# Edges of an attention kernel copied into PSUM by VectorE instead of transposed on TensorE, with other places for its rounds

## The chip, the core and the metric

The kernel runs on one core of a Trainium2 chip, in one launch. The metric is the device time of a run in microseconds (us), and the number to compare is the median of several runs. A profile is one execution, with every instruction's start and length; its span goes from the first instruction to the last.

## The reference

A graph network of four layers on N = 3327 nodes with 128 features, each `x = layernorm(x + layer(x, adj))`. The change touches layer 0, an attention with 128 "batches" d and 8 channels h, where the edge matrix is added to every score:

```python
q = (x @ Wq.T).reshape(d, n, h)          # d = 128, h = 8; k and v alike
a = jnp.einsum('dnh,dmh->dnm', q, k) * d ** -0.5
a = a + adj + adj                        # spatial and edge encoding are both adj
a = jax.nn.softmax(a, axis=2)
out = jnp.einsum('dnm,dmh->dnh', a, v)
```

So there are 128 matrices of 3327 x 3327 scores to be exponentiated; layers 1 to 3 are multiplications with `adj` and its transpose.

## The kernel before

A first stage projects queries, keys and values and writes them to DRAM. The attention stage does layer 0. A last stage does the output projection and layers 1 to 3.

**Blocks.** In attention the queries are cut into 7 chunks of CW = 476 columns (the last one overlaps), the 26 tiles of 128 keys into four sets of 7, 7, 6 and 6 (`KBS`). A chunk with a key set is a block, 28 in all, in the order of chunks. A block goes through d = 0 to 127, in 32 groups of four heads (`GROUP`).

**Scores.** For each d the tiles of the block are done in three sets (`SETS`): 3, 2, 2 tiles of a seven-tile block, 2, 2, 2 of a six-tile block. Each set has its own PSUM banks (`sc`, one buffer each, a bank a tile; seven of the eight banks in all). Scores are not made anew for each d: the bank is never cleared within a block, and the matmul of d adds q_d k_d and takes off q_(d-1) k_(d-1). So the edges are put into the banks once a block, ahead of d = 0, and stay. `exponents` (from L594) does one set: at d = 0 it first transposes the edges into the bank with TensorE (L603), from `e_in`, which has queries in rows; then come the scores (L610); then ScalarE takes the exponential of the whole set in one instruction (L618) into a tile `e0`, `e1` or `e2` of SBUF, with 6, 7 and 8 buffers.

**Help.** In some groups (`on_vector`) VectorE does the exponential of the third set at the group's first d, as a polynomial in ten instructions (`vector_exp`, L574 to L580). The first reads PSUM at once; the others wait in a list `vec`, from which `vector_work` takes some at each place, by a clock of planned costs.

**Rounds.** `weigh` (L624) multiplies one key tile's exponentials of four heads with the values (L635), four matmuls side by side, into the eighth bank `o`. The rounds of a group, 7 or 6, are done during the next group. A group has twelve places, numbered d % 4 times 3 plus the set; a tuple of `PLACES` (L452) lists the places at which rounds follow, and there is one tuple for each g % 4. A round of a third set waits for the polynomial of its group. Every third group, `flush` lets VectorE add `o` into SBUF (L646, L648).

**Order.** In this stage TensorE, ScalarE, VectorE and GpSimd work in program order (`manual_schedule`). `prepare` loads keys and queries two groups ahead on the SP queue (`load_heads`, three buffers), and at d % 4 of 0 or 1 lists the copies of queries for the next group (`copy_queries`, L499 to L501). `load_edges` (L429) loads the edges of the next block at d = 0 of this one, in two DMAs on SP, into the one buffer of `e_in`.

**Background.** While attention runs, the last stage's transposed matrix `adjT_s` is made: every eighth group (`PACE`) a piece of `adj` is loaded on SP, turned by VectorE in blocks of 32 (`piece_work`) and stored by GpSimd's queue (`piece_store`, L234). Row block t of `adjT_s` holds, for the queries of tile t, keys in partitions: the turned edges. Pieces go by four query tiles at a time, tiles 4 on first and tiles 0 to 3 last.

Of the kernel before, what the change touches and what calls it, by code (L numbers as in the profile page):

```python
# [10 lines left out]
F32 = mybir.dt.float32  # L11
# [8 lines left out]
P = 128  # L20
GROUP = 4
# [3 lines left out]
PACE = 8  # L25
CW = 476
# [24 lines left out]
def kernel(ctx: ExitStack, tc: tile.TileContext, x, adj, wq, wk, wv, wo,  # L51
# [14 lines left out]
    nc = tc.nc  # L66
    N, D = x.shape
# [3 lines left out]
    NP = T * P  # L71
# [8 lines left out]
    KBS = [(0, 7), (7, 7), (14, 6), (20, 6)]  # L80
# [40 lines left out]
    adjT_s = scratch.tile([T * P, T * P], F32, name="adjT_s")  # L121
# [123 lines left out]
    with tc.tile_pool(name="pw", bufs=1) as pw, tc.tile_pool(name="pa", bufs=2) as pa, \  # L245
# [12 lines left out]
        for u in range(NU):  # L258
            base, R, full, rest = spread(u)
# [96 lines left out]
        d = 0  # L356
# [52 lines left out]
    def attention():  # L409
        with tc.tile_pool(name="acc", bufs=1) as accp, tc.tile_pool(name="kq", bufs=3) as kq, \  # L410
# [12 lines left out]
            subs = [(j, min(P, CW - j)) for j in range(0, CW, P)]  # L423

            blocks = [(min(c, N - CW), kb) for c in range(0, N, CW) for kb in range(len(KBS))]
            groups = [(b, g) for b in range(len(blocks)) for g in range(NHG)]
            steps = [(b, d) for b in range(len(blocks)) for d in range(D)]

            def load_edges(b):  # L429
                c0, kb = blocks[b]  # L430
                k0, nt = KBS[kb]
                w = min(nt * P, N - k0 * P)
                e = ed.tile([P, len(subs), 7 * P], F32, name="e_in")
                if w < nt * P:
                    nc.gpsimd.memset(e[:, :, w:nt * P], 0.0)
                nf = CW // P
                nc.sync.dma_start(out=e[:, 0:nf, 0:w],
                                  in_=flat_ap(adj, c0 * N + k0 * P, [[N, P], [P * N, nf], [1, w]]))
                nc.sync.dma_start(out=e[0:CW - nf * P, nf, 0:w],
                                  in_=flat_ap(adj, c0 * N + (nf * P * N + k0 * P), [[N, CW - nf * P], [1, w]]))  # L440
                return e


            SETS = {7: [(0, 3), (3, 2), (5, 2)], 6: [(0, 2), (2, 2), (4, 2)]}

            def on_vector(nt, g):

                return g % 4 != 3 if nt == 7 else g % 2 == 0

            PLACES = {7: ((0, 0, 4, 7, 7, 10, 10), (0, 0, 4, 7, 7, 9, 10), (1, 1, 4, 6, 8, 10, 10),  # L452
                          (0, 2, 3, 5, 7, 8, 10)),
                      6: ((0, 0, 3, 6, 8, 10), (0, 2, 4, 5, 7, 9)) * 2}

            def load_heads(b, g):

# [62 lines left out]
            heads, values, pairs, edges, es, stores = {}, {}, {}, {}, {}, []  # L520


            pieces = [(u, c) for u in [*range(1, NU), 0] for c in range(NPC)]
            loaded, worked, turning = [], [], []

            def background(n):
                if n % PACE == 0 and worked:
                    piece_store(pe, *worked.pop(0))
                if n % PACE == 0 and pieces:
                    u, c = pieces.pop(0)  # L530
                    loaded.append((u, c, piece_load(pe, u, c)))

            def background_work(n):
                if n % PACE == 3 and loaded:
# [6 lines left out]
                if n % PACE == 7 and turning:  # L541
                    clock[1] += 2.4
                    for _ in turning.pop():
                        pass
# [38 lines left out]
            clock = [0.0, 0.0]  # L583
# [10 lines left out]
            def exponents(b, d, si):  # L594
                kb = blocks[b][1]
                nt = KBS[kb][1]
                t0, n = SETS[nt][si]
                s = sc[si]
                if d == 0:
                    for i in range(n):  # L600
                        tl = tile_at(nt, t0 + i)[2]
                        for j, (q0, w) in enumerate(subs):
                            nc.tensor.matmul(s[:, i, q0:q0 + w], lhsT=edges[b][0:w, j, tl * P:(tl + 1) * P],  # L603
                                             rhs=ident[0:w, 0:w], is_transpose=True,
                                             start=(j == 0), stop=True, skip_group_check=True)
                kt, qt = heads[b, d // GROUP]
                k = d % GROUP
                for i in range(n):
                    rg, pos, _ = tile_at(nt, t0 + i)
                    nc.tensor.matmul(s[:, i, 0:CW], lhsT=kt[64 * rg:64 * rg + 64, k, pos * P:(pos + 1) * P],  # L610
                                     rhs=qt[64 * rg:64 * rg + 64, k, :],
                                     start=False, stop=True, skip_group_check=True)
                e = ex.tile([P, (3, 2, 2)[si], CW], F32, tag=f"e{si}", name=f"e{si}", bufs=(6, 7, 8)[si])
                if on_vector(nt, d // GROUP) and (d % GROUP, si) == (0, 2):
                    vector_exp(e[:, 0:n, :], s[:, 0:n, 0:CW], (b, d // GROUP))
                    clock[1] += 1.2
                else:
                    nc.scalar.activation(e[:, 0:n, :], s[:, 0:n, 0:CW], AF.Exp, scale=2.0)  # L618
                for i in range(n):
                    es[b, d, t0 + i] = e[:, i, :]  # L620
                if d == 0 and si == len(SETS[nt]) - 1 and b + 1 < len(blocks):
                    edges[b + 1] = load_edges(b + 1)

            def weigh(b, g, r):  # L624

                k0, nt = KBS[blocks[b][1]]
                tl = tile_at(nt, r)[2]
                m = tokens(k0 + tl)
                u = g % PACK

                while any(of == (b, g) for _, of, _ in vec) and r >= SETS[len(queue_of)][2][0]:
                    vec.pop(0)[2]()
                for j in range(GROUP):
                    c = 32 + (tl * GROUP + j) * 32 - u * A1
                    nc.tensor.matmul(o[32 * j:32 * j + 32, 0:CW], lhsT=values[b, g][:m, c:c + 32],  # L635
                                     rhs=es[b, g * GROUP + j, r][:m, :],
                                     start=(r == 0 and u == 0), stop=(r == nt - 1),
                                     skip_group_check=True)
                if r == nt - 1 and (u == PACK - 1 or g == NHG - 1):
                    flush(b, g // PACK)  # L640
# [20 lines left out]
            queue, place = [], 0  # L661
            with tc.manual_schedule(engines={mybir.EngineType.PE, mybir.EngineType.Activation,
                                             mybir.EngineType.Pool, mybir.EngineType.DVE}):
                edges[0] = load_edges(0)
# [472 lines left out]
    with tc.manual_schedule(engines={mybir.EngineType.PE, mybir.EngineType.SP}):  # L1137
# [18 lines left out]
        for t in range(T):  # L1156
            n = tokens(t)
# [87 lines left out]
```

## Time and profile before

| what | value |
|---|---|
| median of 3 runs | 10919.42 us (10911.48 to 10927.48) |
| the profiled execution, its own time | 10915.5 us |
| its span | 10913.7 us |
| first stage / attention / last stage | 334.9 / 9806.6 / 772.2 us |
| exponentials on ScalarE, L618 | 10192, mean 1076 ns |
| exponentials on VectorE, L574 | 560, mean 1150 ns |
| rounds' matmuls, L635 | 46592 records, mean 573 ns |
| scores' matmuls, L610 | 23296, mean 439 ns |
| edges' transposes, L603 | 728, median 272 ns |
| granted TensorE clock | 0.995 |

The page gives busy time for each engine and each group of instructions, and ahead of a group the idle time of its engine with what ended it. Lengths of matmuls and of exponentials overlap in time, so a rate is read from start to start. The timeline lists instructions in order of time, merged where they follow each other, with the idle time before them.

### The profile page before, as it was taken

What the parts mean: (1) busy time and instruction counts of PE and PEld (TensorE: products, weight loads), DVE (VectorE), ACT (ScalarE), POOL (GpSimd) and SP (SyncE); (2) the same over time, 40 slices, a digit from 0 to 9 for tenths busy, and PEclk for the clock granted to TensorE, in tenths of its full rate; (3) what the DMA queues carried; (4) which work ended last, traced back from release to release, by engine and by line L of the source; (5) the groups of instructions that cost most, each with busy time, mean ns of one, the idle gap of its engine ahead of it and who ended that gap; (6) DMA issues with size and microseconds to landing.
All of it is one profiled execution on the core that took longest, in us unless ns stands there. A gap on an engine that the chain in (4) does not pass through costs nothing. (4 is left out here: it accounts for less than half of the span.)

```text
span 10913.7 us, 202710 instructions
## 1 busy us (share of the span) xinstructions
PE 10590.0 (97%) x76941; PEld 4114.5 (38%) x76941; DVE 8351.7 (77%) x9359; ACT 9774.0 (90%) x10671; POOL 1667.9 (15%) x2742
## 2 busy tenths in 40 slices
PE   8899999999999999999999999999999999999999
PEld 5333333333333333333333333333333333333779
DVE  6788778887788877788877888778887788777312
ACT  3799999999999999999999999999999999999400
POOL 0111122111221111211112111121111100001200
PEclk9899999999999999999999999999999999999999
DMA  7888888888888888888888888888888888788676
GB/s 252 155 127 123 129 133 133 128 124 127 136 133 128 124 127 131 136 123 127 131 131 135 115 122 121 123 133 129 126 129 123 120 119 117 116 111 118 209 283 245
DMA packets 995063, 1516.19 MB, mean 139 GB/s; under 512 B 202471, under 2 KB 812577, under 8 KB 980267
## 3 DMA queue, kind: packets, MB, share of 16 engines
q1 hardware_dynamic: 896854, 1371.75, 77.5%
q0 software_dynamic: 79616, 116.88, 4.7%
q8 instruction: 623, 10.21, 0.5%
q10 hardware_dynamic: 17620, 14.49, 0.4%
q14 instruction: 350, 2.87, 0.1%
HBM read 1371.86 MB, written 130.35 MB: 138 GB/s over the span
## 5 line engine op out<-in xcount | busy, mean ns | idle before, releaser
L618 ACT ACTIVATE e<-sc 128x952 f32<-128x952 f32 (+1 forms) x10192 | 9551.3, 1076 | 281.1 <-PE sc L610 274.7
L635 PE MATMUL o<-e,v_pad 128*32 128x476 f32 (+1 forms) x46592 | 5657.5, 573 | 47.1 <-DVE acc L648 39.8
L610 PE MATMUL sc<-qt,kt 64*128 64x476 f32 x23296 | 4503.2, 439 | 178.4 <-ACT e L618 113.1
L610 PEld LDWEIGHTS sc<-qt,kt 64*128 64x128 f32 x23296 | 2197.0, 184 | 4570.9 <-ACT e L618 4015.0
L580 DVE SCALAR_TENSOR_TENSOR e<-e,ey 128x952 f32<-128x952 f32 x1680 | 1932.7, 1150 | 52.3
L515 POOL COPY v_pad<-vs 128x192 f32<-128x192 f32 (+1 forms) x896 | 534.4, 622 | 7986.1 <-DMA vs<-v_img 5559.1
L635 PEld LDWEIGHTS o<-e,v_pad 128*32 128x32 f32 (+1 forms) x46592 | 1027.9, 108 | 1904.7 <-issue 1858.7
L574 DVE TENSOR_SCALAR ey<-sc 128x952 f32<-128x952 f32 x560 | 643.9, 1150 | 1047.2 <-PE sc L610 1041.2
L501 DVE CAST qt<-qt 64x1904 fp32r<-64x1904 f32 x896 | 1032.8, 1153 | 30.4
L499 DVE TENSOR_SCALAR qt<-qt 32x1428 fp32r<-32x1428 f32 x896 | 807.6, 901 | 159.2 <-DMA qt<-q_s 100.6
L234 POOL DMA_DIRECT2D adjT_s<-at x1352 | 785.3, 587 | 234.5 <-DMA adjT_s<-at 162.2
L580 DVE SCALAR_TENSOR_TENSOR e<-e,et 128x952 f32<-128x952 f32 x560 | 647.5, 1156 | 17.8
L576 DVE SCALAR_TENSOR_TENSOR ey<-et,ey 128x952 f32<-128x952 f32 x560 | 645.1, 1152 | 19.4
L580 DVE SCALAR_TENSOR_TENSOR e<-ey 128x952 f32<-128x952 f32 x560 | 642.0, 1146 | 0.0
L1081 PE MATMUL bank<-y,eT 128*128 128x128 f32 (+1 forms) x4056 | 473.9, 276 | 0.4 <-DVE h L1203 0.4
L1081 PEld LDWEIGHTS bank<-y,eT 128*128 128x128 f32 (+1 forms) x4056 | 465.3, 192 | 5.7 <-DVE h L1203 0.6
L648 DVE TENSOR_TENSOR acc<-o,acc 128x476 f32<-128x476 f32 x231 | 150.3, 651 | 312.4 <-PE o L635 312.0
L575 DVE TENSOR_SCALAR et<-ey 128x952 f32<-128x952 f32 x560 | 372.6, 665 | 18.7
L577 DVE TENSOR_SCALAR et<-et 128x952 int32<-128x952 int32 x560 | 371.1, 663 | 19.3
L500 DVE TENSOR_SCALAR qt<-qt 32x476 fp32r<-32x476 f32 x896 | 360.2, 402 | 7.8 <-DMA qt<-lead_s 3.5
L1041 ACT ACTIVATE rstd<-mv,eps 128x1 f32<-128x1 f32 x104 | 30.4, 293 | 265.5 <-DVE mv L1039 265.5
L655 POOL DMA_DIRECT2D o_s<-acc x308 | 191.4, 625 | 34.9 <-DVE acc L648 22.0
(152 smaller groups left out, 2402.6 us busy)
## 6 DMA issues: line engine op xcount, KB each, us to landing
kt<-k_s SPq DMA_DIRECT2D x5320, 96.0 KB
kt<-k_s SPq DMA_DIRECT2D x1764, 128.0 KB
eT<-adjT_s SPq DMA_DIRECT2D x78, 1664.0 KB
qt<-q_s SPq DMA_DIRECT2D x896, 119.0 KB
qt<-q_s SPq DMA_DIRECT2D x1792, 59.5 KB
vs<-v_img SPq DMA_DIRECT2D x224, 224.0 KB
adjT_s<-at POOLq DMA_DIRECT2D x1352, 32.0 KB, 6.0
vs<-v_img SPq DMA_DIRECT2D x224, 192.0 KB
```

Source lines behind the costliest of these rows:

```text
L234: nc.gpsimd.dma_start(out=flat_ap(adjT_s, (t * P + 32 * q) * NP + c * PIECE, [[NP, 32], [P, ns], [1, P]]), in_=at[32 * i:32 * i + 32].rear ...
L499: return [(0.9, None, lambda: nc.vector.tensor_scalar(qt[32:64, 1:], qf[0:32, 0:GROUP - 1], -1.0, None, ALU.mult)), (0.4, None, lambda: nc ...
L501: (1.2, None, lambda: nc.vector.tensor_copy(qt[64:128], qf[0:64]))]
L515: nc.gpsimd.tensor_copy(vp[:, 32:32 + nt * GROUP * 32].rearrange("p (x c) -> p x c", c=32)[:, :, 0:H], vs.rearrange("p (x c) -> p x c", c=H))
L574: nc.vector.tensor_scalar(y, x, -58 * math.log(2.0), 2 / math.log(2.0), ALU.max, ALU.mult)
L575: vec.append((0.7, of, lambda: nc.vector.tensor_scalar(t, y, ROUND, None, ALU.add)))
L576: vec.append((1.2, of, lambda: nc.vector.scalar_tensor_tensor(y, t, ROUND, y, ALU.subtract, ALU.subtract)))
L580: vec.append((1.2, of, lambda i=i, a=a: nc.vector.scalar_tensor_tensor(e, e if i else y, a, t if i == len(POLY) - 1 else y, ALU.add, ALU.m ...
L610: nc.tensor.matmul(s[:, i, 0:CW], lhsT=kt[64 * rg:64 * rg + 64, k, pos * P:(pos + 1) * P], rhs=qt[64 * rg:64 * rg + 64, k, :], start=False ...
L618: nc.scalar.activation(e[:, 0:n, :], s[:, 0:n, 0:CW], AF.Exp, scale=2.0)
L635: nc.tensor.matmul(o[32 * j:32 * j + 32, 0:CW], lhsT=values[b, g][:m, c:c + 32], rhs=es[b, g * GROUP + j, r][:m, :], start=(r == 0 and u = ...
L1081: nc.tensor.matmul(ps[:n, 0:D], lhsT=e[:m, s, :n], rhs=y[:m, s, col:col + D], start=(s == 0), stop=(s == T - 1))
```

## The change

- From the third chunk on (blocks 8 to 27) edges come from `adjT_s`, keys in partitions, and `put_edges` lets VectorE copy them into the banks: three copies a tile, since the chunk doesn't begin at a tile of queries. TensorE's transposes stay for blocks 0 to 7.
- `load_edges` loads one part of the next block's edges at a time, at d = 0, 8, 16, 24 and 32. `e_in` has five row blocks instead of four, `e2` seven buffers instead of eight.
- `on_vector`: of seven-tile groups those with g % 4 of 1, 2, 3 have help (before 0, 1, 2), of six-tile groups the odd ones (before the even ones). As many as before.
- `PLACES` is new; `FIRST` holds for the first group of blocks 1 to 7.
- The background's load and store move from n % 8 = 0 to 2, its work from 3 to 4 and from 7 to 0 of the groups' number.

```diff
-            def load_edges(b):
+            def turned(b):
+                return b >= 2 * len(KBS)
+
+            def put_edges(b, s, i, tl):
+                e = edges[b].rearrange("p t (s n) -> p t s n", n=P)
+                a = blocks[b][0] % P
+                full = (CW + a - P) // P
+                nc.vector.tensor_copy(s[:, i, 0:P - a], e[:, 0, tl, a:P])
+                nc.vector.tensor_copy(s[:, i, P - a:P - a + full * P].rearrange("p (t n) -> p t n", n=P),
+                                      e[:, 1:1 + full, tl, :])
+                rest = CW - (P - a) - full * P
+                if rest:
+                    nc.vector.tensor_copy(s[:, i, CW - rest:CW], e[:, 1 + full, tl, 0:rest])
+                clock[1] += 0.6
+
+            def load_edges(b, j):
...
+                if j == 0:
+                    edges[b] = ed.tile([P, 5, 7 * P], F32, name="e_in")
+                if turned(b):
+                    t = c0 // P + j
+                    if t * P < c0 + CW:
+                        nc.sync.dma_start(out=edges[b][:, j, 0:nt * P],
+                                          in_=flat_ap(adjT_s, t * P * NP + k0 * P, [[NP, P], [1, nt * P]]))
+                    return
...
-                return g % 4 != 3 if nt == 7 else g % 2 == 0
+                return g % 4 != 0 if nt == 7 else g % 2 == 1
...
-            PLACES = {7: ((0, 0, 4, 7, 7, 10, 10), (0, 0, 4, 7, 7, 9, 10), (1, 1, 4, 6, 8, 10, 10),
-                          (0, 2, 3, 5, 7, 8, 10)),
-                      6: ((0, 0, 3, 6, 8, 10), (0, 2, 4, 5, 7, 9)) * 2}
+            PLACES = {7: ((0, 2, 4, 4, 7, 7, 9), (0, 0, 3, 7, 7, 10, 10), (0, 0, 3, 6, 6, 9, 9), (0, 0, 3, 6, 7, 10, 10)),
+                      6: ((0, 2, 4, 6, 8, 10),) * 4}
+
+            FIRST = {7: (4, 4, 5, 7, 7, 10, 10), 6: (4, 4, 7, 7, 10, 10)}
...
                         tl = tile_at(nt, t0 + i)[2]
+                        if turned(b):
+                            put_edges(b, s, i, tl)
+                            continue
...
-                e = ex.tile([P, (3, 2, 2)[si], CW], F32, tag=f"e{si}", name=f"e{si}", bufs=(6, 7, 8)[si])
+                e = ex.tile([P, (3, 2, 2)[si], CW], F32, tag=f"e{si}", name=f"e{si}", bufs=(6, 7, 7)[si])
...
-                if d == 0 and si == len(SETS[nt]) - 1 and b + 1 < len(blocks):
-                    edges[b + 1] = load_edges(b + 1)
+                if d % (2 * GROUP) == 0 and d // (2 * GROUP) < 5 and si == len(SETS[nt]) - 1 \
+                        and b + 1 < len(blocks):
+                    load_edges(b + 1, d // (2 * GROUP))
...
-                        for _ in range(PLACES[len(queue_of)][d // GROUP % 4].count(place) if queue else 0):
-                            weigh(*queue.pop(0))
+                        if queue:
+                            at = PLACES[len(queue_of)][d // GROUP % 4] if d >= GROUP or turned(b) else FIRST[len(queue_of)]
+                            for _ in range(at.count(place)):
+                                weigh(*queue.pop(0))
```

More of the change, by code (lines that the diff above doesn't have):

```diff
@@ L432, in load_edges @@
                 w = min(nt * P, N - k0 * P)
[L433 to L441, printed above, removed]
+                if j == 0:
[6 more added lines that the diff above has]
+                    return
+                if j == len(subs):
+                    return
+                if j == 0 and w < nt * P:
+                    nc.gpsimd.memset(edges[b][:, :, w:nt * P], 0.0)
+                q0, n = subs[j]
+                nc.sync.dma_start(out=edges[b][0:n, j, 0:w],
+                                  in_=flat_ap(adj, (c0 + q0) * N + k0 * P, [[N, n], [1, w]]))
             SETS = {7: [(0, 3), (3, 2), (5, 2)], 6: [(0, 2), (2, 2), (4, 2)]}
             def on_vector(nt, g):
-                return g % 4 != 3 if nt == 7 else g % 2 == 0
-            PLACES = {7: ((0, 0, 4, 7, 7, 10, 10), (0, 0, 4, 7, 7, 9, 10), (1, 1, 4, 6, 8, 10, 10),
-                          (0, 2, 3, 5, 7, 8, 10)),
-                      6: ((0, 0, 3, 6, 8, 10), (0, 2, 4, 5, 7, 9)) * 2}
+                return g % 4 != 0 if nt == 7 else g % 2 == 1
+            PLACES = {7: ((0, 2, 4, 4, 7, 7, 9), (0, 0, 3, 7, 7, 10, 10), (0, 0, 3, 6, 6, 9, 9), (0, 0, 3, 6, 7, 10, 10)),
+                      6: ((0, 2, 4, 6, 8, 10),) * 4}
+            FIRST = {7: (4, 4, 5, 7, 7, 10, 10), 6: (4, 4, 7, 7, 10, 10)}
             def load_heads(b, g):
@@ L526, in background @@
             def background(n):
-                if n % PACE == 0 and worked:
+                if n % PACE == 2 and worked:
                     piece_store(pe, *worked.pop(0))
-                if n % PACE == 0 and pieces:
+                if n % PACE == 2 and pieces:
                     u, c = pieces.pop(0)
@@ L533, in background_work @@
             def background_work(n):
-                if n % PACE == 3 and loaded:
+                if n % PACE == 4 and loaded:
                     u, c, ai = loaded.pop(0)
@@ L540, in background_work @@
                     turning.append(steps)
-                if n % PACE == 7 and turning:
+                if n % PACE == 0 and turning:
                     clock[1] += 2.4
@@ L663, in attention @@
                                              mybir.EngineType.Pool, mybir.EngineType.DVE}):
-                edges[0] = load_edges(0)
+                for j in range(len(subs)):
+                    load_edges(0, j)
                 for n in range(2):
```

## The prediction

> **What bounds the kernel now.** I read the busy shares first, then the stages, then the costly groups, then the timeline of single groups of heads.
>
> ```profile
> PE 10590.0 (97%) x76941; PEld 4114.5 (38%) x76941; DVE 8351.7 (77%) x9359; ACT 9774.0 (90%) x10671; POOL 1667.9 (15%) x2742
> ```
>
> ```profile
> 334.90:10141.50 9806.60, 9581.90 (x70575) 3298.97 (x70577) 7980.60 (x8542) 9551.27 (x10192) 1551.64 (x2626) 1.00 0.84 126
> ```
>
> The second line is the attention stage (columns: length; busy PE, weight load, VectorE, ScalarE, GpSimd; clock, DMA share, GB/s). 9806.6 of 10913.7 us lie there. The change leaves the 335 us ahead and the 772 us behind alone. TensorE looks full, ScalarE nearly so.
>
> ```profile
> L618 ACT ACTIVATE e<-sc 128x952 f32<-128x952 f32 (+1 forms) x10192 | 9551.3, 1076 | 281.1 <-PE sc L610 274.7
> L635 PE MATMUL o<-e,v_pad 128*32 128x476 f32 (+1 forms) x46592 | 5657.5, 573 | 47.1 <-DVE acc L648 39.8
> L610 PE MATMUL sc<-qt,kt 64*128 64x476 f32 x23296 | 4503.2, 439 | 178.4 <-ACT e L618 113.1
> L574 DVE TENSOR_SCALAR ey<-sc 128x952 f32<-128x952 f32 x560 | 643.9, 1150 | 1047.2 <-PE sc L610 1041.2
> L648 DVE TENSOR_TENSOR acc<-o,acc 128x476 f32<-128x476 f32 x231 | 150.3, 651 | 312.4 <-PE o L635 312.0
> ```
>
> ScalarE's idle time is ended by scores (L610). The page's mean of 1076 ns hides that exponentials overlap: start to start, undisturbed, the trace has 0.845 us for two tiles and 1.242 us for three. A group then needs at least, in six-tile blocks, 11 x 0.845 = 9.30 us where VectorE takes one exponential and 10.14 where not; in seven-tile blocks 10.88 and 11.73. Over 14 blocks of each kind that is about 9324 us, against 9807: **some 483 us is ScalarE late**. That is what can be won. Two stretches of ScalarE's timeline show where (start, length, count, idle before):
>
> ```profile
> 5361.90 19.89 ACT L618 ACTIVATE e<-sc 128x952 f32<-128x952 f32 x23 [0.33 <-PE sc L610]
> 5382.12 19.89 ACT L618 ACTIVATE e<-sc 128x952 f32<-128x952 f32 x23 [0.33 <-PE sc L610]
> ```
>
> A stop in each pair of six-tile groups, always at the second exponential of the group with VectorE's help. TensorE there:
>
> ```profile
> 5359.65 1.80 PE L635 MATMUL o<-e,v_pad 128*32 128x476 f32 x16
> 5361.38 0.91 PE L610 MATMUL sc<-qt,kt 64*128 64x476 f32 x6
> 5362.22 1.00 PE L635 MATMUL o<-e,v_pad 128*32 128x476 f32 x8
> ```
>
> x16 is two rounds at one place; the scores behind them start at 5361.38, and ScalarE stands until 5361.90. At a block's start it is the transposes (L603) as well:
>
> ```profile
> 5279.12 0.97 ACT L618 ACTIVATE e<-sc 128x952 f32<-128x952 f32 x1 [2.07 <-PE sc L610]
> 5280.79 4.39 ACT L618 ACTIVATE e<-sc 128x952 f32<-128x952 f32 x5 [0.70 <-PE sc L610]
> ```
>
> The first group of a block loses 3.5 us with seven tiles, 3.1 with six (sum of late starts, medians over blocks). So the bound is the order on TensorE, and the chain of waits, which ends in the tail, says nothing on it.
>
> **The Trainium skill.** "Trainium Kernel Development and Optimization", Performance Expectations, says matmul busy time is a bad measure since matmuls are pipelined; the trace agrees: PE is 97% busy, yet groups differ by 0.4 us with the same matmuls. "VectorE: DVE Perf Modes", Why PSUM operands drop a tier, gives fp32 with a PSUM operand one element per cycle of 0.96 GHz; for reading, L574 agrees (952 elements, 1150 ns, while 952 from SBUF to SBUF at L575 took 665); no row here writes PSUM from VectorE. The same page, Two Vector instructions with no wait between them, lets a next instruction start early; here L580 starts 563 ns after the start of a 647 ns L648. "PSUM — Partial Sum Buffer", The four PSUM rules, says VectorE's writes leave the accumulation bits as they are, so scores with start=False add to copied edges where bits are set; that needs no extra instruction.
>
> **A rule for the order, from start times.** A bank is free for new scores 1.01 us after its two-tile exponential starts (1.40 for three tiles). Scores must start 0.53 us before their exponential (0.75 for three tiles). Scores to the next scores: 0.32 us behind a round, 0.21 otherwise; a round between them adds about 1.03, a second one at the same place 0.80; a group's first scores cost 0.28 more, waiting for separate loads. Checked on before, six tiles, group with help, zero at its first exponential: scores 0 at -1.48, two rounds, scores 1 at 0.84, needed at 0.845-0.53=0.32: late 0.52; measured 0.507. Next stop by the rule 0.10, measured 0.077. Seven tiles with two rounds first: 0.13 against 0.115 measured.
>
> **Part 1: places and VectorE's groups.** Six tiles, new order (0,2,4,6,8,10). Group with help: scores 0 at -1.48, one round, scores 1 at 0.05 (in time), scores 2 at 0.37, round, scores 3 at 1.61. VectorE took exponential 2, so exponential 3 is due at 1.69 and needs scores at 1.17: late 0.445. Nothing after it is late. Group without help: none late. Pair: 0.445 for the measured 0.61+0.18=0.79, so **-0.345**. Seven tiles, the new four orders: 0, 0.125, 0.42 (two rounds at place 10 ahead push it 0.39), 0.125, with 0.03 of small ones: 0.70, for measured 0.155+0.59+0.36+0.20=1.30, so **-0.60 per four groups**. Over 31 groups a block and 14 blocks of each kind: 0.345x15.5x14=75 and 0.60x7.75x14=65, together 140 us. Costs set at nothing, with cover: the seventh instead of eighth buffer of e2 (the last round ends some 0.6 us before the exponential that needs it); the polynomial of help, which ended 2.6 us into the next group in the trace, while the first round needing it comes at about 5.5; background work moved one group on, with the groups without help that cover it.
>
> **Part 2: edges, 20 of 28 blocks.** Removed: 28 or 24 transposes at about 0.104 us of issue. Added on VectorE: three copies a tile, 476 elements: 476/0.96=0.496 us, plus 3 x 0.072 (0.157 fixed of a row such as 652-496, less the 0.085 overlap): 0.71 us a tile. Bounds: 0.46 if it ran at two elements a cycle, 1.06 without overlap (3 x (0.157+0.03)+0.496); the planner's 0.6 is a price, not a measurement. Copies start when the first bank is free, 1.53 us ahead of the block's first due exponential, and run on in order; the third exponential starts 0.55 after the last tile. Due at 2.09 (seven tiles): late 7x0.71-1.53+0.55-2.09=1.9; six: 6x0.71-1.53+0.55-1.69=1.6. VectorE is not always free just then (help in seven-tile groups started 0.4 to 0.6 late, the rest of an instruction 0 to 1.15): +0.5. So 2.4 and 2.1 for 3.5 and 3.1: about 1.05x20=**-21 us**. Behind the waiting copies stand the last polynomial's steps and the next queries; group 0 is now without help, and VectorE's work there (4.2 left of a polynomial, 4.3 to 5 of copies, 2.4 of queries, 2.4 of background) fits its 14 us. Late next: the scores, by 0.53 a bank.
>
> **Part 3: FIRST, blocks 1 to 7.** Without rounds before place 4 the transposes hide under exponentials: by the rule 1.3 late with seven (0.65 behind the first 12 transposes, 0.43 and 0.19 behind the rounds bunched at places 4, 5 and 7) and 2.4 with six (0.45 behind transposes, the rest behind seven rounds bunched likewise), for 3.5 and 3.1: 3x2.2+4x0.7=**-9 us**.
>
> **Part 4: loads.** Edges are at most 2.3 instead of 1.7 MB a block, in four or five loads over nine groups instead of two at once, on the same SP queue between the heads' loads; an issue is 0.3 to 0.4 us. Group 2 of the first seven-tile block of a chunk is 1.3 us long in most chunks where others aren't; I put **-5 us** on the burst going. The DRAM reads wait for stores that ended many groups ago.
>
> Sum 175: from this execution's 10915.5 (span 10913.7) to 10740; the median of runs is 3.9 higher, so 10745.
>
> **Rivals.** (1) TensorE's throughput is the limit, not its order: 97% busy speaks for it, equal matmuls in unequal groups against. Then transposes give 2.7x20=54, one more change between scores and rounds per six-tile pair costs 0.235x15.5x14=51, three fewer per four seven-tile groups give 76: -79, 10840. (2) **Slower:** copies into PSUM, which no row shows, become the wait: each extra us a tile costs 6.5x20=130 us at block starts, in series with ScalarE. From 0.71+175/130=2.05 us a tile the change loses; at 2.5 it gives 10980. For it: three small instructions, each with its waits; against: reading PSUM is at full rate. (3) Stops only move (round 2 of a six-tile group now stands before scores 3) and parts 2 to 4 alone remain: 10890. (4) That edges still come through TensorE in late chunks is excluded by the code.
>
> **Numbers.** Mine 0.60, rival 1 0.14, rival 2 0.13, rival 3 0.13. My own range is 10660 to 10850 (the copy's bounds give -33 and +46; 0.1 us a group wrong in the rule gives 87); with rivals 1 and 3 the range is 10660 to 10900. A measurement tells 0.2%, 22 us, from no change. Rival 3 is split between faster and same: faster 0.79, same 0.07, slower 0.14.
>
> **What would show it.** Right: transposes 208 instead of 728; ScalarE's idle time before L618 under 200 us; six-tile pairs near 19.9 us; copies of some 0.7 us a tile. Wrong: VectorE copies over 1.5 us a tile, scores waiting on VectorE at every block start for over 4 us, a new stop at place 3 above 0.8, or loads arriving late.

## The result: slower by 0.6%, and the profile after

| kernel | median of runs | against before, in the same comparison |
|---|---|---|
| before | 10923.45 us (4 runs) | |
| after | 10987.15 us (4 runs, 10984.25 to 10989.82) | **1.0059 [1.0041, 1.0076]** |

The profiled execution took 10984.25 us, its span is 10982.5. The forecast was 10745, faster; the kernel became 64 us slower.

The page's shares and groups (busy time and mean ns; then idle time ahead, with what ended it), page of after:

```profile
PE 10609.2 (97%) x76421; PEld 4098.7 (37%) x76421; DVE 8520.5 (78%) x9749; ACT 9768.3 (89%) x10671; POOL 2004.4 (18%) x2737
...
L647 ACT ACTIVATE e<-sc 128x952 f32<-128x952 f32 (+1 forms) x10192 | 9546.5, 1111 | 354.6 <-PE sc L639 275.9
L665 PE MATMUL o<-e,v_pad 128*32 128x476 f32 (+1 forms) x46592 | 5667.5, 576 | 9.0 <-DVE acc L678 2.4
L639 PE MATMUL sc<-qt,kt 64*128 64x476 f32 x23296 | 4561.8, 444 | 272.5 <-issue 82.8
```

L647 is the exponential (L618 before), L639 the scores, L665 the rounds. ScalarE's idle time grew from 281.1 to 354.6, where under 200 was forecast. TensorE lost 520 transposes and its share still reads 97%: that share showed neither kernel's bound. The attention stage of after (length, busy times, clock, DMA share, GB/s) is 69.2 us longer than before, as much as the whole difference between the two spans (68.8):

```profile
335.10:10210.90 9875.80, 9599.45 (x70049) 3281.47 (x70052) 8149.16 (x8932) 9546.41 (x10192) 1888.00 (x2621) 0.99 0.85 126
```

Its clock column went from 1.00 to 0.99, the whole kernel's from 0.995 to 0.986. Summed as in the prediction (each exponential's start beyond 0.845 or 1.242 us after the one before it), ScalarE is late by 552.0 us instead of 482.8: again 69.2. By blocks, the time sits in one place. From the start of one block to the next, blocks 0 to 7, whose edges still go through TensorE, mostly took about 370.2 us with seven tiles and 324.5 with six (before: 369.4 to 370.2, and 328.7 to 329.3). Blocks 8 to 27, whose edges VectorE copies, took 376 and 332. The loss is at the twenty starts of those blocks: the first group of such a block is late by 8.7 us (seven tiles) and 8.3 (six) on the average, for 3.5 in before.

The start of block 8, timeline of VectorE in after (start, length, operation, count):

```profile
3115.12 3.52 DVE L606 SCALAR_TENSOR_TENSOR e<-e,ey 128x952 f32<-128x952 f32 x3
3118.55 0.23 DVE L438 COPY sc<-e_in 128x72 f32<-128x72 f32 x1
3118.82 0.56 DVE L439 COPY sc<-e_in 128x384 f32<-128x384 f32 x1
3119.41 0.18 DVE L443 COPY sc<-e_in 128x20 f32<-128x20 f32 x1
3119.63 0.24 DVE L438 COPY sc<-e_in 128x72 f32<-128x72 f32 x1
...
3121.58 0.18 DVE L443 COPY sc<-e_in 128x20 f32<-128x20 f32 x1
3121.67 0.23 DVE L438 COPY sc<-e_in 128x72 f32<-128x72 f32 x1
...
3125.64 0.18 DVE L443 COPY sc<-e_in 128x20 f32<-128x20 f32 x1
```

By the prediction's rule the first bank is free at about 3116.45 (1.01 us after its last exponential starts, a two-tile one of the six-tile block 7), but VectorE is inside the polynomial of that block's last group (L606), so the first copy starts 2.1 us later. A tile takes 1.08 us from start to start (3118.55 to 3119.63), not 0.71, and the three pieces of a tile don't overlap: 3118.82 + 0.56 is 3119.38, and the next starts at 3119.41. Seven tiles take 7.27 us. TensorE at the same place, in after:

```profile
3116.23 0.48 PE L639 MATMUL sc<-qt,kt 64*128 64x476 f32 x2
3121.86 1.13 PE L639 MATMUL sc<-qt,kt 64*128 64x476 f32 x3 [5.16 <-issue]
3122.92 1.81 PE L665 MATMUL o<-e,v_pad 128*32 128x476 f32 x8
```

TensorE stands for 5.16 us, until the third tile of the first set is copied: the scores of a set start only after the set's last copy (ended 3121.76). And then a round, which takes 1.00 elsewhere, takes 1.81. The view by windows says why; its last columns are clock, DMA share and GB/s:

```profile
3107.40:3117.60 10.20, 8.28 (x62) 2.39 (x60) 8.63 (x10) 8.99 (x11) 0.00 (x0) 1.00 0.90 131
3120.60:3130.80 10.20, 8.40 (x36) 2.53 (x36) 9.65 (x22) 4.42 (x4) 3.10 (x6) 0.50 0.96 147
```

For 10.2 us, from the last 1.3 us of the gap on, **the granted clock is 0.50**, and TensorE, busy for 8.40 us in it, gets through 36 records where it did 62 in the window before. ScalarE there, in after:

```profile
3112.04 6.11 ACT L647 ACTIVATE e<-sc 128x952 f32<-128x952 f32 x7 [0.90 <-PE sc L639]
3123.08 1.36 ACT L647 ACTIVATE e<-sc 128x1428 f32<-128x1428 f32 x1 [4.93 <-PE sc L639]
3125.47 0.96 ACT L647 ACTIVATE e<-sc 128x952 f32<-128x952 f32 x1 [1.03 <-PE sc L639]
3126.77 0.96 ACT L647 ACTIVATE e<-sc 128x952 f32<-128x952 f32 x1 [0.34 <-PE sc L639]
3129.67 11.23 ACT L647 ACTIVATE e<-sc 128x1428 f32<-128x1428 f32 x11 [1.93 <-PE sc L639]
```

Idle 4.93, then 1.03, 0.34 and 1.93. The last is the first exponential of the next d, which needs no edges any more: it waits behind rounds at half clock. Every one of the twenty starts has a gap of 3.27 to 5.18 us on TensorE, and a stretch at half clock that begins in the gap or within 1 us of its end.

### The profile page after: what moved, and what is told of

Its sections match the earlier page's. It is cut to its first block, busy times and chain, and to the rows that moved or that the text cites. A ratio compares the mean times of both kernels' runs of the same rounds, so it can differ in the third digit from the quotient of the medians.

```text
span 10982.5 us, 202713 instructions
## 1 busy us (share of the span) xinstructions
PE 10609.2 (97%) x76421; PEld 4098.7 (37%) x76421; DVE 8520.5 (78%) x9749; ACT 9768.3 (89%) x10671; POOL 2004.4 (18%) x2737
## 5 line engine op out<-in xcount | busy, mean ns | idle before, releaser
L647 ACT ACTIVATE e<-sc 128x952 f32<-128x952 f32 (+1 forms) x10192 | 9546.5, 1111 | 354.6 <-PE sc L639 275.9
L665 PE MATMUL o<-e,v_pad 128*32 128x476 f32 (+1 forms) x46592 | 5667.5, 576 | 9.0 <-DVE acc L678 2.4
L639 PE MATMUL sc<-qt,kt 64*128 64x476 f32 x23296 | 4561.8, 444 | 272.5 <-issue 82.8
L639 PEld LDWEIGHTS sc<-qt,kt 64*128 64x128 f32 x23296 | 2220.7, 185 | 4696.7 <-ACT e L647 3973.3
L541 POOL COPY v_pad<-vs 128x192 f32<-128x192 f32 (+1 forms) x896 | 738.1, 849 | 7758.9 <-DMA vs<-v_img 5942.2
L606 DVE SCALAR_TENSOR_TENSOR e<-e,ey 128x952 f32<-128x952 f32 x1680 | 1935.8, 1152 | 51.9
L665 PEld LDWEIGHTS o<-e,v_pad 128*32 128x32 f32 (+1 forms) x46592 | 1040.8, 108 | 1899.8 <-issue 1868.9
L234 POOL DMA_DIRECT2D adjT_s<-at x1352 | 852.6, 637 | 198.8 <-DMA adjT_s<-at 157.2
L606 DVE SCALAR_TENSOR_TENSOR e<-e,et 128x952 f32<-128x952 f32 x560 | 653.6, 1167 | 17.7
L606 DVE SCALAR_TENSOR_TENSOR e<-ey 128x952 f32<-128x952 f32 x560 | 640.6, 1144 | 0.0
L685 POOL DMA_DIRECT2D o_s<-acc x308 | 258.4, 843 | 30.4 <-DVE acc L678 20.6
```

What stands on the lines that cost most here:

```text
L234: nc.gpsimd.dma_start(out=flat_ap(adjT_s, (t * P + 32 * q) * NP + c * PIECE, [[NP, 32], [P, ns], [1, P]]), in_=at[32 * i:32 * i + 32].rear ...
L541: nc.gpsimd.tensor_copy(vp[:, 32:32 + nt * GROUP * 32].rearrange("p (x c) -> p x c", c=32)[:, :, 0:H], vs.rearrange("p (x c) -> p x c", c=H))
L606: vec.append((1.2, of, lambda i=i, a=a: nc.vector.scalar_tensor_tensor(e, e if i else y, a, t if i == len(POLY) - 1 else y, ALU.add, ALU.m ...
```

## The experiments

My theory (A in the expectations): the copies cost some 6.8 us at each of the twenty starts, by their length, by VectorE's lateness and by the half clock; the rest of the change gains. Its rivals blame the new places, or the part loads. Each kernel is after with the edit shown, and "against after" compares differences to before, each in its own comparison, since before itself differed by up to 12 us between comparisons.

| kernel | median us | ratio to before | against after |
|---|---|---|---|
| e1: edges through TensorE in all blocks | 10848.56 | 0.9941 [0.9928, 0.9955] | -127 |
| e2: places of before | 11033.27 | 1.0111 [1.0096, 1.0126] | +58 |
| e3: three rounds ahead of the first scores | 10966.72 | 1.0050 [1.0036, 1.0064] | -8 |
| e4: last polynomial steps behind the copies | 10982.22 | 1.0063 [1.0049, 1.0077] | +7 |
| e6: TensorE kept busy in the gap | 10971.83 | 1.0054 [1.0040, 1.0068] | -7 |
| e7: one copy a tile | 10928.54 | 1.0013 [1.0006, 1.0019] | -51 |
| e11: e7 and TensorE kept busy | 10896.31 | 0.9981 [0.9973, 0.9988] | -84 |
| e8: e1 without `FIRST` | 10870.90 | 0.9962 [0.9948, 0.9976] | -108 |
| e10: e1, edges loaded at once | 10857.69 | 0.9946 [0.9932, 0.9959] | -123 |
| e5: e1, seven-tile places of before | 10833.22 | 0.9928 [0.9914, 0.9941] | -146 |
| e9: e5, another six-tile order | 10862.50 | 0.9951 [0.9937, 0.9964] | -118 |

**e1: edges through TensorE.** `FIRST` then holds for all blocks.

```diff
-                return b >= 2 * len(KBS)
+                return False
```

> The changed kernel with edges transposed on TensorE in all 28 blocks; its orders of rounds, help, FIRST and loads in parts stay. Theory A (the copies on VectorE at block starts cost the time: TensorE waits there for 3.3 to 5.2 us and then runs 10 us at half clock): blocks 8 to 27 take what blocks 0 to 7 take in the changed kernel, 370 us with seven tiles and 324.6 with six, so some 75 us less than before, 10850, and no half clock windows at block starts. Rival B (the new orders cost the time): no better than before, 10920 or more.

With the copies gone (and `FIRST` in their blocks, which e8 prices) a loss of 0.6% becomes a gain of 0.6%. Timeline of TensorE at the start of block 8, in e1 (L632 is the transposes):

```profile
3115.50 0.49 PE L639 MATMUL sc<-qt,kt 64*128 64x476 f32 x2
3115.92 1.45 PE L632 MATMUL sc<-ident,e_in 128*128 128x128 f32 x12
3117.30 0.70 PE L639 MATMUL sc<-qt,kt 64*128 64x476 f32 x3
```

Twelve transposes fill the three banks of the first set in 1.45 us, and TensorE has no gap. The three groups from a block's last one to its second took 35.0 and 37.1 us in e1 (first and second seven-tile block of a chunk) against 42.6 and 43.9 in after; 34.6 and 32.0 against 41.7 and 37.9 with six. That is 6.8 us a start on the average, 136 in all, beside 127 in the medians and 133 in the spans. ScalarE's idle time in e1 (view of groups):

```profile
L647 ACT ACTIVATE e<-sc 128x952 f32<-128x952 f32 (+1 forms) x10192 | 9544.5, 1111 | 221.7 <-PE sc L639 214.7 <-ACT e L647 0.2
```

**e2: places of before,** moved by one group as the help is; copies and `FIRST` stay.

```diff
-            PLACES = {7: ((0, 2, 4, 4, 7, 7, 9), (0, 0, 3, 7, 7, 10, 10), (0, 0, 3, 6, 6, 9, 9), (0, 0, 3, 6, 7, 10, 10)),
-                      6: ((0, 2, 4, 6, 8, 10),) * 4}
+            PLACES = {7: ((0, 2, 3, 5, 7, 8, 10), (0, 0, 4, 7, 7, 10, 10), (0, 0, 4, 7, 7, 9, 10),
+                          (1, 1, 4, 6, 8, 10, 10)),
+                      6: ((0, 2, 4, 5, 7, 9), (0, 0, 3, 6, 8, 10)) * 2}
```

> The changed kernel with the orders of rounds of before, shifted by one group so that each falls to a group with the same help as before; copies, FIRST and loads in parts stay. Theory A: the copies' loss stays and the six-tile gain of 4.2 us a block goes: 10987+59-10, about 11035. Rival B: faster than the changed kernel, 10900 or less.

So the new places don't cause the loss; they win 58 us where the copies are. Part of the 58 may be the clock's: half clock covers 348.8 us of this execution and 303.4 of after.

**e3: rounds into the gap.** In blocks with copies, three rounds are done ahead of the first scores, and the first three places of that group are dropped.

```diff
+                        if d == 0 and si == 0 and turned(b):
+                            for _ in range(3):
+                                weigh(*queue.pop(0))
                         exponents(b, d, si)
...
+                            at = at[3:] if d < GROUP and turned(b) else at
```

> The changed kernel with three rounds of the group before done ahead of the first scores of blocks 8 to 27 (the same work in another place), so TensorE works 2.6 us of its idle time there. Theory A with the clock as a part of the loss: gaps stay under 2.6 us, the half clock windows at block starts vanish, and some 2.5 us a block come back: 10935. Rival (the clock costs nothing, VectorE sets all): windows may vanish, the time stays within 15 us, 10975 to 10990.

It moved in the direction expected, by far less, and the interval doesn't separate it from after. Timeline of TensorE at block 8, in e3:

```profile
3115.70 2.60 PE L665 MATMUL o<-e,v_pad 128*32 128x476 f32 x24
3120.89 0.70 PE L639 MATMUL sc<-qt,kt 64*128 64x476 f32 x3 [2.59 <-DVE sc L443]
3122.92 0.67 PE L639 MATMUL sc<-qt,kt 64*128 64x476 f32 x2 [1.33 <-DVE sc L443]
3125.04 1.52 PE L639 MATMUL sc<-qt,kt 64*128 64x476 f32 x5 [1.45 <-DVE sc L443]
```

The one gap became three, of 2.59, 1.33 and 1.45, and the clock still fell (the five scores at 3125.04 take 1.52, where after shows 0.92 for five at full clock, at 3131.26). Half clock covers 279.5 us of this execution, 303.4 of after and 116.4 of before. My expectation that short gaps keep the clock up was wrong: at blocks 10 and 14 no gap was longer than 1.64 us, there were three near each other, and half clock followed.

**e4: copies first.** No polynomial steps are taken at a block's last d if the next block is copied.

```diff
-                while vec and clock[1] < clock[0]:
+                while vec and clock[1] < clock[0] and not hold:
...
-                        vector_work(b)
+                        vector_work(b, d == D - 1 and turned(b + 1))
```

> The changed kernel with the polynomial's remaining steps held back in the last d of a block that a copied block follows, so that VectorE is free when the first bank is. Theory A with VectorE's lateness as a part (the first copy began 2.1 us after its bank was free in block 8): about 1.8 us a block, 10950, and TensorE's idle gap shrinks by as much. Rival (only the copies' length and the wait for whole sets count): within 10 us of the changed kernel, 10980 to 10995.

No difference that can be measured. The mechanism was there: in block 8 the first copy came 0.93 us after the bank was free instead of 2.11, and the first exponential 3.9 late instead of 5.1. But the postponed steps came back: in the copied blocks the first group was less late by 0.6 us, and the second, group 1, later by about as much (1.52 instead of 0.64 with seven tiles, 1.70 instead of 1.21 with six); all late starts sum to 550.4 instead of 552.0. VectorE's work in that stretch was postponed, not saved.

**e6: TensorE busy in the gap.** Five rounds (four with six tiles) with weights of zero are added to `o` ahead of the first scores, in blocks with copies.

```diff
...
+                        if d == 0 and si == 0 and turned(b):
+                            for _ in range(KBS[blocks[b][1]][1] - 2):
+                                for j in range(GROUP):
+                                    nc.tensor.matmul(o[32 * j:32 * j + 32, 0:CW], lhsT=nought,
+                                                     rhs=edges[b][:, 0, 0:CW], start=False, stop=False,
...
                         exponents(b, d, si)
```

> The changed kernel with TensorE kept busy while it waits at the start of blocks 8 to 27: five (seven tiles) or four (six tiles) rounds whose weights are all zero, added to the sums in bank o, ahead of the first scores. They add work and change nothing in the output. Theory A (half clock is a part of the loss): no half clock windows at block starts, and some 2 us a block come back although work was added: 10947. Rival (half clock costs nothing since VectorE sets the pace there): unchanged or slower, 10985 or more.

In time the step can't be told from none. The trace says why it is small: half clock fell from 303.4 us to 170.2, most windows from 10.2 to 3.4, but the later gaps (behind the second and third set's copies) still brought some. Where a block had none, the three groups at its start took 42.2 us instead of 43.9 (seven tiles), 39.3 instead of 41.7 (six): 1.7 to 2.4 us a window, with the added matmuls paid.

**e7: one copy a tile.** The loads put the 476 queries of a tile next to each other in SBUF (at most 512 bytes a piece), and each tile is one copy.

```diff
+            def straight(b):
+                return edges[b].rearrange("p t c -> p (t c)")[:, 0:7 * CW].rearrange("p (s q) -> p s q", q=CW)
...
+                nc.vector.tensor_copy(s[:, i, 0:CW], straight(b)[:, tl, :])
...
-                        nc.sync.dma_start(out=edges[b][:, j, 0:nt * P],
-                                          in_=flat_ap(adjT_s, t * P * NP + k0 * P, [[NP, P], [1, nt * P]]))
+                        q0, q1 = max(c0, t * P), min(c0 + CW, t * P + P)
+                        nc.sync.dma_start(out=straight(b)[:, 0:nt, q0 - c0:q1 - c0],
+                                          in_=flat_ap(adjT_s, t * P * NP + k0 * P + q0 - t * P,
+                                                      [[NP, P], [P, nt], [1, q1 - q0]]))
```

> The changed kernel with the turned edges loaded so that a tile's 476 queries lie side by side (pieces of at most 512 bytes in the DMA), and one copy a tile instead of three. Theory A (the copies stand in series with ScalarE at block starts, 1.08 us a tile): a tile takes 0.69, 20 blocks x 6.5 tiles x 0.395 = 51 us less: 10936. Rival (the copies' length is hidden, only the wait for VectorE and the half clock count): within 15 us of the changed kernel, 10972 or more.

VectorE's timeline at block 8, in e7:

```profile
3117.90 4.53 DVE L438 COPY sc<-e_in 128x476 f32<-128x476 f32 x7
```

4.53 us for seven tiles instead of 7.27, and 51 us of the kernel: three pieces a tile, with what follows from their length, cost two fifths of what the copies lost. A tile takes 0.68 us here, slightly less than the 0.71 of the prediction, and the kernel still doesn't gain on before: the copy's length alone doesn't explain the miss.

**e11: e7, and four (three) zero-weight rounds.**

```diff
+                            for _ in range(KBS[blocks[b][1]][1] - 3):
```

> e7_one_copy with TensorE kept busy while it waits at the start of blocks 8 to 27: four or three rounds with zero weights ahead of the first scores, as in e6_busy_wait. Theory A (copies, their three instructions and the half clock are parts that add up): the half clock windows at block starts vanish and some 1.5 us a block come back, 10898; what is left over e1_tensor_only, 50 us, is one copy a tile and VectorE's lateness. Rival (with short copies the half clock no longer counts): 10920 or more.

Here the gaps are closed, and no block start has a window. TensorE at block 8, in e11 (L707 is the zero-weight rounds):

```profile
3117.90 0.48 PE L638 MATMUL sc<-qt,kt 64*128 64x476 f32 x2
3118.31 3.40 PE L707 MATMUL o<-e_in,nought 128*32 128x476 f32 x32
3122.37 0.67 PE L638 MATMUL sc<-qt,kt 64*128 64x476 f32 x3 [0.66 <-issue]
3122.97 1.01 PE L664 MATMUL o<-e,v_pad 128*32 128x476 f32 x8
```

The gap is 0.66 and the round behind it takes 1.01. The only edit to e7 is matmuls that add nothing, and it wins 33 us: the half clock has a price of its own, 1.7 us a start in e7. ScalarE's idle time in e7 and in e11, which falls by as much:

```profile
L644 ACT ACTIVATE e<-sc 128x952 f32<-128x952 f32 (+1 forms) x10192 | 9544.0, 1117 | 303.3 <-PE sc L636 270.6 <-DMA qt<-q_s 25.8 <-ACT e L644 0.2
```

```profile
L646 ACT ACTIVATE e<-sc 128x952 f32<-128x952 f32 (+1 forms) x10192 | 9544.8, 1117 | 269.6 <-PE sc L638 236.0 <-DMA qt<-q_s 26.0 <-ACT e L646 0.2
```

With this the 127 us between after and e1 divide, step by step, into 51 for one copy instead of three, 33 for the half clock that was left then, and 43 that stay even with one copy a tile at full clock. The first two are not copy and clock apart: with the shorter gaps, half clock already fell from 303.4 us in after to 229.3 in e7 (122.8 in e11), so a part of the 51 is the clock's, and which part no run shows. The 43 sit at the first exponential of a block, late by 3.2 us with seven tiles and 2.2 with six in e11, by 0.9 and 0.3 in e1: some 41 us over the twenty starts. The copies of the first set and VectorE's late start (1.5 to 2.1 us in e7 too) both lie in there; I didn't divide them.

**e8: e1 without `FIRST`.**

```diff
-                            at = PLACES[len(queue_of)][d // GROUP % 4] if d >= GROUP or turned(b) else FIRST[len(queue_of)]
+                            at = PLACES[len(queue_of)][d // GROUP % 4]
```

> All edges on TensorE as in e1_tensor_only, without FIRST: the first group of a block uses the common orders. Theory A (FIRST hides the transposes under exponentials, as costed in the prediction: 2.2 us a block with seven tiles, 0.7 with six): 40 us more than e1_tensor_only, 10889. Rival (the order of the first group hardly matters): within 10 us, 10840 to 10860.

`FIRST` is worth 18 to 22 us over 27 blocks, some 0.7 to 0.8 a block, half of what was expected. The first group improves (3.43 to 2.05 us late with seven tiles, 3.18 to 2.15 with six, means of blocks 1 to 27), but group 1 takes part of it back (0.26 to 0.50, 0.51 to 0.98): the rounds put off come later.

**e10: e1 with all edges of the next block loaded at its d = 0.**

```diff
-                if d % (2 * GROUP) == 0 and d // (2 * GROUP) < 5 and si == len(SETS[nt]) - 1 \
-                        and b + 1 < len(blocks):
-                    load_edges(b + 1, d // (2 * GROUP))
+                if d == 0 and si == len(SETS[nt]) - 1 and b + 1 < len(blocks):
+                    for j in range(5):
+                        load_edges(b + 1, j)
```

> e1_tensor_only with the edges of the next block loaded all at once at d = 0, as before, instead of in parts. The prediction's part 4: 5 us more than e1_tensor_only, 10854. Rival (the loads hide either way): within 3 us of e1_tensor_only.

0.9946 and e1's 0.9941 overlap widely: what loading in parts brings, if anything, stays open.

**e5: e1 with the seven-tile places of before,** moved by one group; the six-tile places stay new.

```diff
-            PLACES = {7: ((0, 2, 4, 4, 7, 7, 9), (0, 0, 3, 7, 7, 10, 10), (0, 0, 3, 6, 6, 9, 9), (0, 0, 3, 6, 7, 10, 10)),
+            PLACES = {7: ((0, 2, 3, 5, 7, 8, 10), (0, 0, 4, 7, 7, 10, 10), (0, 0, 4, 7, 7, 9, 10), (1, 1, 4, 6, 8, 10, 10)),
```

> All edges on TensorE as in e1_tensor_only, and the seven-tile orders of rounds those of before, shifted by one group; the six-tile order stays new. Theory A (the new seven-tile order loses: late starts of 1.42 us per four groups in the changed kernel, 1.30 in before): 13 us less than e1_tensor_only by the medians, up to 24 by the whole blocks, so 10825 to 10836, the fastest so far. Rival (the new seven-tile order gains 0.6 us per four groups, as predicted): 65 us more, 10913.

**The fastest of all, ahead of before by 0.72%.** The new seven-tile places cost time: they are 19 us behind the old ones. The two intervals overlap, but the blocks tell them apart: with seven tiles most took 368.7 to 369.4 us here and 369.8 to 370.9 in e1, with six about 324.6 in both.

**e9: e5 with before's order in the helped six-tile groups,** and the new one in the others.

```diff
-                      6: ((0, 2, 4, 6, 8, 10),) * 4}
+                      6: ((0, 2, 4, 6, 8, 10), (0, 0, 3, 6, 8, 10)) * 2}
```

> e5_old_seven (edges on TensorE, seven-tile orders of before) with a mixed six-tile order: groups with help take the order of before, (0,0,3,6,8,10), groups without help keep the new one. Theory A (late starts add up by group: 0.61 in the first kind with the order of before for 0.69 with the new one, 0 in the second kind with the new one): 0.08 us a pair of groups, 15.5 pairs, 14 blocks, 17 us less than e5_old_seven: 10816. Rival (the order of a group without help is late behind the other's): no gain or a loss, 10830 or more.

I expected the best half of each order to add up; it lost 28 us against e5, at the six-tile blocks, most of which took 326.4 to 327.3 us for 324.6. ScalarE in six-tile groups, timelines of e5 and then of e9:

```profile
2498.48 19.81 ACT L647 ACTIVATE e<-sc 128x952 f32<-128x952 f32 x23 [0.30 <-PE sc L639]
2518.59 12.10 ACT L647 ACTIVATE e<-sc 128x952 f32<-128x952 f32 x14 [0.30 <-PE sc L639]
```

```profile
2480.50 19.88 ACT L647 ACTIVATE e<-sc 128x952 f32<-128x952 f32 x23 [0.84 <-PE sc L639]
2500.71 19.99 ACT L647 ACTIVATE e<-sc 128x952 f32<-128x952 f32 x23 [0.33 <-PE sc L639]
2521.04 9.60 ACT L647 ACTIVATE e<-sc 128x952 f32<-128x952 f32 x11 [0.34 <-PE sc L639]
```

From stop to stop 20.11 us in e5, 20.21 and 20.33 in e9. The helped group with two rounds first stops for 0.68 us at its second exponential, where the same order stopped 0.507 in before; there the neighbour's last round was at place 9, here it is at place 10. My reading, which no run isolates, is that the round at place 10 still delays the next group's first scores.

## Why the prediction was wrong

The sum was -175 us and the measurement +64. By the runs, 135 of the 239 us between them are in Part 2, 100 in Parts 1 and 4, and 3 or 4 in Part 3.

**Part 2, edges: -21 forecast, +114 measured** (after against e8 is +108, and after has `FIRST` in seven blocks, 6 us). This is the step that failed and turned the sign: copies were to make a block's start cheaper, 2.4 and 2.1 us late, and made it 8.7 and 8.3 us late. The form of its sum held. With seven tiles the copies' length, less 1.53, plus 0.55, less 2.09, plus VectorE's lateness, gives with block 8's terms 7.27 - 1.53 + 0.55 - 2.09 + 2.11 = 6.3; its first three exponentials were late by 5.1 + 1.15 + 0.46 = 6.7. (The 0.4 more: at half clock the third set's exponential starts 0.80 after its scores, 3125.97 to 3126.77, and the scores 0.15 after the copy.) Three terms were wrong. (So was a figure of before that set out the gain: the first group of a six-tile block lost 3.5 us there, not 3.1; that would have raised the forecast by some 4 us.)
- *Copies of 0.71 us a tile* were 1.08. Fixed cost and rate were right (128x384 took 561 ns and 128x20 took 182, so 1.04 ns an element and 0.16 fixed), but the overlap of 0.085 taken from L580 behind L648 didn't exist between pieces of one tile; they stand 0.03 apart. The upper bound, 1.06 without overlap, was nearly the measured value. The Trainium skill, "VectorE: DVE Perf Modes", allows an early start in Two Vector instructions with no wait between them. Here a wait is what tells the copies apart: in the trace's records each further copy of a set carries a wait for a semaphore that VectorE's own instructions raise, and none of these 330 started early; the first copy of the second and third set carries one for ScalarE's semaphore alone, and all 40 did (3121.67, where the one before ends at 3121.76). L580 behind L648 has a wait for VectorE's semaphore as well, perhaps for an older instruction, which the records don't tell. So that the copies into one tile wait for each other is a reading that no run isolates.
- *VectorE late by 0.5* was 1.5 to 2.1 over the twenty blocks. The prediction knew that help moves to the odd groups, and so into a block's last group; it counted the polynomial's 4.2 us as work that fits in 14 us, and not as what stands ahead of the copies. That moving the steps doesn't help, e4 shows.
- *What comes after the copies* was priced at nothing. The first exponential of the next d was late by another 2.05 (seven tiles) and 1.66 (six), most of it, it seems, since TensorE ran at half clock: with short copies it is 1.16 and 1.66 in e7, which still has some half clock, and 0.78 and 0.57 in e11 at full clock (medians). The Trainium skill, "TensorE: Matmul & The Clock Gate", Why this matters for your kernels, warns of TensorE idle for more than about 3 us between bursts; the prediction has no term for the clock and never asked what TensorE does while VectorE copies. The gaps agree with the page in after (3.27 to 5.18 us, all twenty with half clock) and go beyond it in e3, where no single gap reached 3 us.

How the terms share the loss, e7 and e11 show in part: with copies at the forecast length (0.68 us a tile) the kernel is still 76 us behind e1, whose first groups, 2.0 and 2.1 us late, are about what was forecast for the copies. So the two terms that the prediction held small or at nothing weigh more than the mis-sized copy.

**Rival 2** named this mechanism, copies in series with ScalarE, and ended on the right side. Its point of decision was wrong: 2.05 us a tile was worked out against a gain of 175 us, of which all but Part 2's 21 came to 51. With 72 for 175, the same sum puts the point at about 1.26, and the measured 1.08 still lies below it: what decided was VectorE's lateness and the clock, which its price left out. **Rival 1**, TensorE's throughput as the limit, finds no support: e1 gives TensorE its 520 transposes back and is 127 us faster than after.

**Part 1, places, with Part 4: -145 forecast, -45 measured** (e8 against before; the seventh buffer of `e2`, the shifted help and the shifted background work, priced at nothing, are in it, and no run takes them apart). The six-tile half went the right way: the helped group stops only at place 3, as forecast, but for 0.68 us instead of 0.445 (why stays open), and the other not at all. A pair from stop to stop takes 20.11 us in after:

```profile
2503.84 19.81 ACT L647 ACTIVATE e<-sc 128x952 f32<-128x952 f32 x23 [0.30 <-PE sc L639]
2523.95 19.81 ACT L647 ACTIVATE e<-sc 128x952 f32<-128x952 f32 x23 [0.29 <-PE sc L639]
```

Before it took 20.22, and 19.9 was forecast; stops of 0.35 in every third pair, which nobody had counted, went as well. Late starts fell from a mean 0.92 a pair to 0.71, about 46 us for the forecast 75. The seven-tile half went the wrong way: a mean 1.78 us per four groups after against 1.53 before (groups 4 to 31), where the rule gave 0.70 against 1.30. Its two largest stops (medians) are 0.43 at place 1 of g % 4 = 2, which the rule had as 0.42, and 0.36 at place 7 of the same group, behind two rounds at place 6, which it had as nothing. The rule was checked on three stops ahead of time, none of them behind a pair of rounds in the middle of a group; e5 gained by taking the seven-tile orders back. **Rival 3**, stops that only move, came nearest for the places: a six-tile pair's stops moved to place 3 and lost a quarter, the seven-tile ones grew.

**Part 3** was about right (0.7 to 0.8 us a block in e1 against e8, so -5 to -6 for seven blocks instead of -9). **Part 4** stayed unresolved.

Of the signs named beforehand, transposes x208 came true, six-tile pairs, ScalarE's idle time and the copies' 0.7 us a tile missed, and the sign of being wrong, scores waiting over 4 us at a block's start, was there in every copied seven-tile block (4.31 to 5.18).

## What to carry to other kernels

When work leaves an engine, ask what that engine does while the other one works: here TensorE went from 1.45 us of transposes to 5 us of nothing, and paid for it again at half clock afterwards. Price a handed-over step from its first free input to its last output, at the instant it runs, with the upper bound for every small instruction and with whatever stands ahead of it on its new engine. An order that helps one shape of group should be taken for that shape alone and measured there: the two halves of `PLACES` had opposite signs, and halves of two good orders didn't add up.

## What the runs showed of the hardware that I hadn't expected

- **Half clock in steps of 3.4 us.** At the starts of blocks 8 to 27 in after it lasted 10.2 us seventeen times, 6.8 twice and 3.4 once, and up to 13.7 in e2, although TensorE was soon at work again.
- **No length of gap came out as safe.** In before, gaps of 1.55 and 1.60 us brought no half clock, and the only stretch in mid-attention (6058.3 us) went with a gap of 8.4. But in e5 one gap of 1.51 us (from 7277.7) brought 3.4 us of it, and in e7 one of 2.48, at the start of block 26, brought 6.8.
- **Matmuls that add nothing kept the clock up:** up to 3.4 us of them at each start turned a loss into a gain (e7 to e11, 1.0013 to 0.9981).
- **VectorE writes fp32 into PSUM about as fast as it reads it:** 476 elements in 652 ns, where L648 of before, which reads as many from PSUM, took 651. View of groups by form, in e7:

```profile
L438 DVE COPY sc<-e_in 128x476 f32<-128x476 f32 x130 | 81.2, 652 | 2.4
```
